# A wait for sixteen small transfers, moved from inside a group of products to the front of a dense group ahead of it

## The chip, the cores and the metric

The kernel runs on one core of a Trainium2 chip. Its engines are TensorE (matrix products into PSUM), VectorE, ScalarE, GpSimd and SyncE, each with an instruction stream of its own; they meet through semaphores. The metric is the device time of one execution in microseconds, and of several runs their median.

## What is computed

The input x has 16 images of 56 x 56 pixels with 384 channels, in float32. Two layers follow one another:

```python
x = x + L0_conv(gn(x), w_qkv, w_out, b_out, rel_pos_table)   # attention in shifted windows of 7 x 7
x = x + L1_conv(gn(x), w)                                    # 3 x 3 convolution of each channel alone
```

`gn` is a group normalization over 32 groups. In the first layer the image is rolled by 3 pixels, `q, k, v` come from one product with `w_qkv`, are cut into 12 heads of 32 channels and into windows of 49 pixels, and for each head and window

```python
score = einsum("qd,kd->qk", q, k) / sqrt(32) + rel      # some windows are masked at the image's edges
out   = einsum("qk,kd->qd", softmax(score), v)
```

is projected with `w_out`. The change concerns how `v` comes to the second of these products.

## The kernel before

**Tiling.** An image has 8 strips of 7 rows, each strip 8 windows. The 16 images give 128 strips. A strip is worked on in two units of four windows, so there are 256 units; unit u belongs to strip u // 2, and units with an even number are the first of their strip. Channels lie on the partitions in three blocks of 128.

**Order of the work.** The whole program is written out by hand: each engine does its instructions in the order in which the code issues them. `heavy` (L937) lists the work of one unit in six slots, mainly for TensorE. In the even unit of strip s it holds, for the strip after it, s + 1:

- slots 0, 1, 2: `value(s + 1, m)` (L481), the products that make v of channel block m: three products of 128 x 128 x 392 into one PSUM bank, which ScalarE then copies to `vt`.
- slots 1, 2, 3: `turn(s + 1, m)` (L494), a transpose of 32 x 32 blocks by VectorE from `vt` to `vq`, which brings keys onto partitions.
- slots 3, 4, 5: `query_key(s + 1, m)` (L469), the first three of the six blocks of q and k.
- behind slot 3 and behind slot 5: `by_key(s + 1, part)` (L501), eight DMAs each on SyncE's queue (L508). They bring `vq` into `v` of the strip, with the 49 keys of a window on consecutive partitions. Each DMA holds the values of one head in four and of one group of 32 keys. `v` has two buffers.

In the odd unit the slots hold the other three blocks of `query_key` for s + 1, then `project` (L647), the output projection of the finished strip s into `py`; VectorE adds x to it (L664) and takes its statistics (L670).

`all_units` (L971) goes through the units. Behind slot 0 of each it puts the rest of the attention of this unit: `add_up` (L589), 32 small product passes that sum the exponentials (L597); `invert` (L631), where ScalarE (L635, L636) and VectorE (L637, L638) invert the sums; `attend` (L606), 96 passes of small products of 49 x 32 x 49 with `v` (L617); and `divide` (L641). So the products with `v` of strip s in its even unit stand behind the first value group of strip s + 1, and they are some six slots and a whole unit behind the issue of the DMAs that fill `v` of strip s. Scores for the next unit (`scores`, L513) and its softmax (L535, L543, L558) come behind slot 2 or 3.

**Work between.** `at` (L899) puts further work into slots by hand-set due times: the loads of the next image (`fetch_halves`, `turn_halves` L435, `arrange` L440 with copies by ScalarE and statistics at L452) and the convolution of the image before: `band` (L698, a DMA on SyncE's queue), `pad` (L733), eight `tap`s for each chunk on VectorE (L780, L784), a transpose in place (`turn_sum`, L788, L791) and eight DMAs for each chunk out to memory (`store`, L793, L798), again on SyncE's queue. That queue issues in the program's order.

**Waits.** The framework gives each engine and each of eight DMA lanes a semaphore, and sets a wait wherever an instruction depends on another engine's or a DMA's work that its engine has not waited for yet. The sixteen DMAs of a strip are spread over the eight lanes. In the kernel before, the first eight products of `attend` in the even unit wait for the DMAs that carry their own head and keys.

Of the kernel before, what the change touches and what calls it, by code (L numbers as in the profile page):

```python
# [34 lines left out]
def kernel(  # L35
# [12 lines left out]
    nc = tc.nc  # L48
# [42 lines left out]
    def bank(name):  # L91
        return ps.tile([P, 512], F32, tag="mm", name=name)
# [388 lines left out]
    def value(s, m):  # L481

        pv = bank(f"pv_{s}_{m}")
        for c in range(NC):
            nc.tensor.matmul(  # L485
                pv[:, :ST].rearrange("p (w t) -> p w t", t=T),
                wq_t[:, c, 2 * C + m * P : 2 * C + (m + 1) * P],
                xn[:, c, :, :T],
                start=(c == 0),
                stop=(c == NC - 1),  # L490
            )
        nc.scalar.copy(vt[:, m, :, :T], pv[:, :ST].rearrange("p (w t) -> p w t", t=T))  # L492

    def turn(s, m):  # L494
# [3 lines left out]
            vt[:, m].rearrange("p (n w) (j b) -> p n (w j) b", w=2, b=D),  # L498
        )

    def by_key(s, part):  # L501

        if part == 0:
            vs[s] = vpool.tile([P, NW // 2, C], F32, tag="v", name=f"v_{s}")
        v = vs[s]
        for half in range(2 * part, 2 * part + 2):
            for i in range(HPC):
                nc.sync.dma_start(  # L508
                    v[half * D : (half + 1) * D].rearrange("k n (m c) -> k (n m) c", m=NC)[:, :, i * D : (i + 1) * D],
                    vq[i * D : (i + 1) * D, half].rearrange("k n m d -> k (n m) d"),  # L510
                )

    def scores(u, fast):  # L513


        s, n = divmod(u, UPS)
        pp = ps_s.tile([P, HPC, 512], F32, tag="s", name=f"ps_{u}")
        for j in range(NC):
            for w in range(2):
                for r in range(2):  # L520
                    for i in range(HPC):
                        part = slice(i * D, (i + 1) * D)
                        q0 = (n * UW + 2 * r + w) * T
                        row, col = (w, r) if fast else (r, w)
                        k0 = (2 * j + col) * T
                        nc.tensor.matmul(  # L526
                            pp[row * HT : (row + 1) * HT, i, k0 : k0 + T],
                            qk[part, NC * fast + j, q0 : q0 + HT],
                            qk[part, NC * (not fast) + j, q0 : q0 + T],
                            start=True,  # L530
                            stop=True,
                        )
        raw[u] = pp
# [403 lines left out]
    def heavy(u):  # L937

        s, half = divmod(u, UPS)
        todo = [[] for _ in range(2 * NC)]  # L940
        more = s + 1 < B * NS
        for m in range(NC):
            if half == 0 and more:
                todo[m].append((value, (s + 1, m)))
                todo[m + 1].append((turn, (s + 1, m)))
                todo[NC + m].append((query_key, (s + 1, m)))
            if half and more:
                todo[m].append((query_key, (s + 1, NC + m)))
            if half:
                todo[NC + m].append((project, (s, m)))  # L950
        if more and not half:
            for part in range(2):
                todo[NC + 2 * part].append((by_key, (s + 1, part)))
        if half and s + 2 < B * NS:
            todo[NC + 1].append((normalize, (s + 2,)))
        return todo
# [14 lines left out]
    def all_units(fast):  # L971
# [4 lines left out]
        for m in range(NC):  # L976
            value(0, m)
# [4 lines left out]
        for part in range(2):  # L982
            by_key(0, part)
# [142 lines left out]
```

## Time and profile before

| | |
|---|---|
| median of 3 runs | 4131.12 us |
| lowest and highest run | 4129.32 and 4135.01 us |
| profiled execution (its span; the page tells no other time of it) | 4128.7 us |
| busy: TensorE, VectorE, ScalarE, GpSimd | 4041.2, 3495.7, 2237.9, 1875.3 us |
| TensorE's clock over the span | 0.99 of full |
| values, L485: products and mean of one | 2304 passes, 497 ns |
| products with the values, L617 | 24576 passes, 212 ns |
| transfers of the values, L508 | 2048, of 48 KB |

Instructions overlap on TensorE, so that the duration of one small product says little of what it adds to the time. The distance from the start of one group to the start of the next says more, and the timeline has it. A semaphore step (EVENT_SEMAPHORE) counts as no busy time.

### The profile page before, as it was taken

How to read it: one execution, taken by the hardware profiler on the slowest of the kernel's cores; microseconds unless marked ns; L12 is line 12 of the kernel's file. 1: busy time of each engine (PE TensorE's matmuls, PEld its weight loads, DVE VectorE, ACT ScalarE, POOL GpSimd, SP SyncE). 2: the span in 40 equal slices, each digit the busy share in tenths (PEclk: the TensorE clock that was granted, in tenths of full speed). 3: DMA queues.
4: the chain of work that ended last, by engine and by line, in shares of the span. 5: the costliest groups of instructions: out<-in, count | busy, mean ns of one | idle time of the engine just before them, and what ended most of it. 6: DMA issues, size and time to landing. Idle time of an engine off the chain costs nothing.

```text
span 4128.7 us, 153178 instructions
## 1 busy us (share of the span) xinstructions
PE 4041.2 (98%) x67257; PEld 2554.0 (62%) x67257; DVE 3495.7 (85%) x3711; ACT 2237.9 (54%) x4654; POOL 1875.3 (45%) x3165
## 2 busy tenths in 40 slices
PE   5999999999999999999999999999999999999997
PEld 3666666666666666666666666666666666666656
DVE  4555989889898998989889898988989889898897
ACT  2545646555565655655555564655556555564552
POOL 5444435545453554445445453554545455452000
PEclk8999999999999999999999999999999999999998
DMA  4434556555665665556555555665556565554544
GB/s 94 79 60 90 110 100 126 105 109 103 116 114 108 116 113 103 110 98 127 106 115 108 109 116 103 117 115 100 114 100 121 104 122 109 101 121 77 107 100 109
DMA packets 1524022, 439.45 MB, mean 106 GB/s; under 512 B 1458970, under 2 KB 1473979, under 8 KB 1523346
## 3 DMA queue, kind: packets, MB, share of 16 engines
q1 hardware_dynamic: 1432680, 267.66, 38.1%
q0 software_dynamic: 87648, 159.12, 15.7%
q8 instruction: 531, 8.70, 0.9%
q10 hardware_dynamic: 3018, 2.78, 0.3%
q14 instruction: 145, 1.19, 0.1%
HBM read 169.63 MB, written 158.46 MB: 79 GB/s over the span
## 4 chain that ended last, share of the span: by engine, by line
PE 68%; issue 10%; DVE 9%; POOL 7%; DMA 4%; ACT 1%; SPq 1%; DVEq 0%; ACTq 0%; POOLq 0%
PE pq L472 28%; PE pv L485 14%; PE py L656 13%; PE ps L526 6%; PE po L617 5%; POOL xl L419 5%; DVE o L784 4%; PE ps L597 3%; DMA xl<-in_x_dram 1%; DMA mvd<-mv 1%; DVE e L543 1%; SPq L508 1%; POOL dev L268 1%; DVE st L452 1%; DVE y L664 1%
## 5 line engine op out<-in xcount | busy, mean ns | idle before, releaser
L472 PE MATMUL pq<-xn,wq_t 128*128 128x392 f32 x4608 | 1587.5, 497 | 0.1
L419 POOL DMA_DIRECT2D xl<-in_x_dram x1980 | 1331.2, 722 | 162.1 <-DVE xt L436 99.6
L784 DVE SCALAR_TENSOR_TENSOR o<-hp,dw_t,o 128x1568 f32<-128x1568 f32 x752 | 1378.4, 1833 | 5.4
L472 PEld LDWEIGHTS pq<-xn,wq_t 128*128 128x128 f32 x4608 | 846.6, 188 | 596.5 <-issue 1.9
L485 PE MATMUL pv<-xn,wq_t 128*128 128x392 f32 x2304 | 814.5, 497 | 4.7 <-DVE y L664 3.5
L656 PE MATMUL py<-ot,wo_t 128*128 128x392 f32 x2304 | 816.1, 499 | 3.0 <-DVE ot L645 3.0
L479 ACT COPY qk<-pq 128x392 f32<-128x392 f32 x768 | 369.9, 483 | 661.1 <-PE pq L472 660.1
L676 POOL COPY y<-y 128x63 f32<-128x63 f32 x128 | 54.5, 426 | 1314.6 <-DVE y L664 1314.6
L656 PEld LDWEIGHTS py<-ot,wo_t 128*128 128x128 f32 x2304 | 427.4, 190 | 298.0 <-DVE ot L645 6.9
L485 PEld LDWEIGHTS pv<-xn,wq_t 128*128 128x128 f32 x2304 | 423.6, 188 | 304.1 <-DVE y L664 5.3
L561 ACT ACTIVATE e<-e 128x1176 f32<-128x1176 f32 x256 | 303.2, 1185 | 417.9 <-DVE e L543 416.9
L637 DVE SCALAR_TENSOR_TENSOR ln<-ps,inv 128x588 f32<-128x588 f32 x256 | 195.9, 765 | 386.0 <-ACT inv L636 381.2
L492 ACT COPY vt<-pv 128x392 f32<-128x392 f32 x384 | 189.3, 493 | 431.6 <-PE pv L485 430.9
L526 PEld LDWEIGHTS ps<-qk 32*64 32x64 f32 x24576 | 308.5, 131 | 144.3 <-issue 123.0
L617 PE MATMUL po<-e,v 49*32 49x49 f32 x24576 | 368.9, 212 | 8.8 <-DMA v<-vq 7.9
L617 PEld LDWEIGHTS po<-e,v 49*32 49x32 f32 x24576 | 357.9, 105 | 16.4 <-issue 8.8
L543 DVE SCALAR_TENSOR_TENSOR e<-ps,bias 128x1176 f32<-128x1176 f32 x256 | 347.3, 1357 | 14.2 <-PE ps L526 13.9
L526 PE MATMUL ps<-qk 32*64 32x49 f32 x24576 | 340.7, 225 | 1.7 <-DVE ln L637 1.6
L448 ACT COPY x<-xt 128x196 f32<-128x196 f32 x720 | 225.6, 368 | 173.8 <-DVE xt L436 173.6
L496 DVE STREAM_TRANSPOSE vq<-vt 128x512 f32<-128x512 f32 x384 | 265.8, 693 | 8.9 <-ACT vt L492 5.4
L664 DVE TENSOR_TENSOR y<-py,x 128x392 f32<-128x392 f32 x384 | 213.2, 555 | 51.2 <-PE py L656 47.9
L461 ACT ACTIVATE xn<-x,coef 128x392 f32<-128x392 f32 x384 | 247.1, 711 | 14.5 <-DMA coef<-cod 14.5
(173 smaller groups left out, 3349.6 us busy)
## 6 DMA issues: line engine op xcount, KB each, us to landing
v<-vq SPq DMA_DIRECT2D x2048, 48.0 KB
xb<-mid SPq DMA_DIRECT2D x90, 855.5 KB
out_dram<-o SPq DMA_DIRECT2D x736, 98.0 KB
mid<-y POOLq DMA_DIRECT2D x112, 619.5 KB
xl<-in_x_dram POOLq DMA_DIRECT2D x1260, 52.5 KB
mid<-y POOLq DMA_DIRECT2D x15, 354.0 KB
xl<-in_x_dram POOLq DMA_DIRECT2D x180, 28.0 KB
mid<-y POOLq DMA_DIRECT2D x15, 265.5 KB
```

The source lines that it names most:

```text
L419: nc.gpsimd.dma_start(xz[i * D + lo : i * D + hi, c, k : k + n, :], flat[token : token + n * (hi - lo)].rearrange("(k t) c -> t k c", k=n) ...
L472: nc.tensor.matmul(pq[:, :ST].rearrange("p (w t) -> p w t", t=T), wq_t[:, c, m * P : (m + 1) * P], xn[:, c, :, :T], start=(c == 0), stop=( ...
L479: nc.scalar.copy(qk[:, m, :ST], pq[:, :ST])
L485: nc.tensor.matmul(pv[:, :ST].rearrange("p (w t) -> p w t", t=T), wq_t[:, c, 2 * C + m * P : 2 * C + (m + 1) * P], xn[:, c, :, :T], start= ...
L496: nc.vector.transpose(vq[:, :, :, m].rearrange("p h n d -> p n h d"), vt[:, m].rearrange("p (n w) (j b) -> p n (w j) b", w=2, b=D),)
L526: nc.tensor.matmul(pp[row * HT : (row + 1) * HT, i, k0 : k0 + T], qk[part, NC * fast + j, q0 : q0 + HT], qk[part, NC * (not fast) + j, q0 ...
L543: nc.vector.scalar_tensor_tensor(e, pp[:, :, : NC * 2 * T].rearrange("q i (n k) -> q i n k", k=T), QSCALE, bias[:, int(s % NS == NS - 1)]. ...
L561: nc.scalar.activation(flat, flat, AF.Exp, accum_out=reach[:, 0, u : u + 1])
L617: nc.tensor.matmul(po[w][i * D : (i + 1) * D, (2 * j + r) * T : (2 * j + r + 1) * T], vs[s][keys, n * 2 + r, h * D : (h + 1) * D], by_head ...
L656: nc.tensor.matmul(py[:, :ST], wo_t[:, c, m * P : (m + 1) * P], ots[s][:, c, :], start=(c == 0), stop=(c == NC - 1),)
L664: nc.vector.tensor_tensor(view.rearrange("p r (w c) -> p w r c", c=WIN), py[:, :ST].rearrange("p (w r c) -> p w r c", r=WIN, c=WIN), xs[s] ...
L784: nc.vector.scalar_tensor_tensor(acc, by_half(hp[:, dy : dy + BR, dx : dx + W]), dw_t[:, c, t : t + 1], acc, ALU.mult, ALU.add)
```

## The change

The DMAs of `by_key` are written down by strip. When the first product of a strip's values is issued (`c == 0` of the first block m), it is given a dependency on all sixteen DMAs of the strip before, that is, of the strip whose products with the values follow behind this group. This holds from the third strip's values on (`s > 1`). The first strip's products keep their waits, and so do the last strip's, which have no value group ahead of them.

```diff
             stop=(c == NC - 1),
             )
+            if c == 0:
+                for name in carried.pop(s - 1, ()) if s > 1 else ():
+                    tc.add_manual_dep(
+                        product.ins,
+                        name,
+                        mybir.DependencyInfo(mybir.DependencyClass.Sync, mybir.DependencyReason.DATA),
+                        reason="values of the strip ahead",
+                    )
...
+    carried = {}
 
     def by_key(s, part):
...
-                nc.sync.dma_start(
+                move = nc.sync.dma_start(
                     v[half * D : (half + 1) * D].rearrange("k n (m c) -> k (n m) c", m=NC)[:, :, i * D : (i + 1) * D],
                     vq[i * D : (i + 1) * D, half].rearrange("k n m d -> k (n m) d"),
                 )
+                carried.setdefault(s, []).append(move.ins.name)
```

No instruction changes its place in any engine's order, and no buffer changes.

More of the change, by code (lines that the diff above doesn't have):

```diff
@@ L484, in value @@
         for c in range(NC):
-            nc.tensor.matmul(
+            product = nc.tensor.matmul(
                 pv[:, :ST].rearrange("p (w t) -> p w t", t=T),
```

## The prediction

> **What bounds the kernel now.** I read the page first, then the groups of line L617, then the timelines of TensorE, of SyncE's DMA queue and of VectorE. The page says which engine sets the time:
>
> ```profile
> PE 4041.2 (98%) x67257; PEld 2554.0 (62%) x67257; DVE 3495.7 (85%) x3711; ACT 2237.9 (54%) x4654; POOL 1875.3 (45%) x3165
> L485 PE MATMUL pv<-xn,wq_t 128*128 128x392 f32 x2304 | 814.5, 497 | 4.7 <-DVE y L664 3.5
> L617 PE MATMUL po<-e,v 49*32 49x49 f32 x24576 | 368.9, 212 | 8.8 <-DMA v<-vq 7.9
> ```
>
> TensorE is busy 98% of the span and hardly ever idle in front of the values (L485) or the products with them (L617), so a microsecond given to or taken from its stream is a microsecond of the kernel. But busy is not the same as fast: a sequencer that steps through waits in the middle of overlapping small products leaves no idle time in this view. The answer for line L617 shows such steps:
>
> ```profile
> L617 PEldq EVENT_SEMAPHORE  x949: 51/51/51, 87.9 to 4012.4; - x190
> ```
>
> The timeline of TensorE in the strip that starts at 2006 prices them. Both of its units do the same 32 sums (L597) and 96 products (L617); only the first unit meets the new strip's values:
>
> ```profile
> 2006.33 2.14 PE L485 MATMUL pv<-xn,wq_t 128*128 128x392 f32 x6
> 2008.39 0.73 PE L597 MATMUL ps<-e,ones 49*32 49x147 f32 x32
> 2008.93 1.66 PE L617 MATMUL po<-e,v 49*32 49x49 f32 x96
> 2010.51 4.22 PE L485 MATMUL pv<-xn,wq_t 128*128 128x392 f32 x12
> ...
> 2024.01 0.73 PE L597 MATMUL ps<-e,ones 49*32 49x147 f32 x32
> 2024.54 1.28 PE L617 MATMUL po<-e,v 49*32 49x49 f32 x96
> 2025.75 4.22 PE L472 MATMUL pq<-xn,wq_t 128*128 128x392 f32 x12
> ```
>
> From the first sum to the next dense group: 2.12 us in the even unit, 1.74 us in the odd one. That 0.38 us is what the waits cost. All 949 wait steps lie in even units (8 in 98 strips, 6 in 13, 7 in one, 5 in 16); the odd units have none, so the program drops a wait that TensorE has already passed.
>
> The other question is when the transfers land, seen against the place where the change puts the wait. SyncE's queue in the strip whose values start at 1944.40, and TensorE's first weight load of the next strip's values:
>
> ```profile
> 1961.85 5.77 SPq L508 DMA_DIRECT2D v<-vq  x8
> 1967.66 3.01 SPq L798 DMA_DIRECT2D out_dram<-o  x4
> 1970.71 6.30 SPq L508 DMA_DIRECT2D v<-vq  x8
> ```
> ```profile
> 1975.21 1.83 PEld L485 LDWEIGHTS pv<-xn,wq_t 128*128 128x128 f32 x6
> ```
>
> The last of the sixteen transfers is issued at about 1976.4 and its semaphore is full at 1978.57, both after the group that is to wait for them has begun. The reader is to see that this needs no theory of the hardware: the wait is put ahead of the issue. Why they are late is in VectorE's timeline:
>
> ```profile
> 1951.19 0.73 DVE L637 SCALAR_TENSOR_TENSOR ln<-ps,inv 128x588 f32<-128x588 f32 x1
> 1961.12 0.67 DVE L496 STREAM_TRANSPOSE vq<-vt 128x512 f32<-128x512 f32 x1
> 1965.13 0.77 DVE L637 SCALAR_TENSOR_TENSOR ln<-ps,inv 128x588 f32<-128x588 f32 x1 [0.21 <-ACT inv L636]
> ```
>
> VectorE runs without a gap up to the third turn (1961.12), 16.7 us after the strip's start, and SyncE issues in order: eight transfers, four stores of the convolution, eight transfers. In the strip of 2006.00, where VectorE has no backlog, the first transfer starts 12.3 us in.
>
> **What the Trainium skill says.** (1) "Perfetto Trace Analysis", Identifying Dependency Chains: an instruction that waits for several engines may get EventSemaphore instructions with the further conditions ahead of it. The trace agrees: those are the 949 steps of 51 ns. (2) "TensorE: Matmul & The Clock Gate", table at its head: TensorE's queue is 64 deep. The trace agrees in kind: the one such step that the values already have stands at 2002.12, 3.9 us ahead of its product, under queued dense products. (3) "DMA: Bandwidth & Descriptors", Rules for kernel authors: issue early and wait on the semaphore late. The change waits earlier than before. (4) The TensorE page, Part 1: after an idle window of about 3.4 us the clock falls to half. The trace's clock records stand at 0.5 from 88.7 to 98.9 us, behind a 5.4 us wait for the same transfers.
>
> **The change part by part.** Durations are of the profiled execution (span 4128.7 us; the runs' median is 4131.12, so 2.4 us is added for what lies around it).
>
> *Removed: the waits inside the products*, in 126 strips (the first keeps them, the change starts at the second; the last has no value group after it). Measured from the first sum to the last product's end, medians: 2.18 us with 8 steps, 2.03 with 7, 1.92 with 6, 1.80 with 5; 1.81 in odd units. So five steps hide under the sums and each further one costs about 0.12 us. Sum over the 126: 37.7 (96 strips with 8) + 1.6 + 0.2 + 0.1 = **39.5 us**. It contains the few short waits for late landings in there. Bounds: 37 (96 x 0.37 + 13 x 0.11), and 44 if measured to the start of the next dense group.
>
> *Added: the wait steps in front of the values.* Eight semaphores, so four to eight steps of 51 ns, at most 0.4 us. Ahead of them are twelve queued passes of the output projection (L656), 4.2 us of work. Where the landings are there, they cost nothing; without that cover it would be 126 x 0.4 = 50 us, which the step at 2002.12 speaks against.
>
> *Added: the wait itself.* Queued behind it on TensorE is everything: values, sums, products, scores. For each of 126 strips I took the last semaphore update of its sixteen transfers and the start of the next strip's first value weight load. **53 are late, by 88.5 us in sum**: 23 by under 1 us, 10 by 1 to 2, 8 by 2 to 3, 12 by 3 to 3.9. In 18 even the issue begins after TensorE is there. It follows the convolution's place in a batch (8 strips): medians for strips 0 to 7 -5.2, +0.7, +1.5, -0.7, 0.0, +3.2, -3.3, -1.9 us (plus is late). Until now the products came 2.9 us after that point and most of the lateness lay under the first value group and the sums. With the median landing (2.17 us behind the issue) for all the sum is 78.
>
> *Does a stall help the next strip?* Stalled by d, TensorE starts its next value group d later, while VectorE works off its backlog, so the next transfers are less late by up to that backlog: what stands between the first unit's inverse (ScalarE) and L637 is 0.03 to 2 us. Against this TensorE arrives 0.37 us sooner from the faster products. Carried from strip to strip with these numbers the sum is 90.7; with no carry 88.5, with full carry into one next strip 91.7. The pattern explains it: the big deficits stand before strips with room. I take **88**.
>
> *Restart.* From a semaphore's last update to the product behind a wait step the trace has some 135 ns (update, step's end 79 ns later, weight load, product), and a cold first dense product takes 597 instead of 490 ns; the weight load that I count from leads its product by 0.33 us, which hides most. Up to three more steps: 0.1 us x 53 = **5 us** (0 to 10).
>
> *Clock.* Some 20 stalls are over 2 us. The trace has a 2.25 us idle stretch (4037.6 to 4039.9) with the half clock from 4041.3, and a 3.04 us one (4080.4 to 4083.4) without. A half-clock window of 3.4 us costs 1.7 us. None to twenty of them: 0 to 34 us; I take five, **8 us**, since the dense work on both sides fills part of each window.
>
> *Moved or untouched.* No DMA, copy or turn is moved, and no queue is passed; `add_manual_dep` changes waits alone. What is late next after the products: 13 times value group two waited for VectorE's eviction (3.5 us in all); in a stalled strip that is past by then, so I cost it at nothing; if not, at most 13 x 0.37 = 5 us of the gain is lost.
>
> Sum: 4128.7 - 39.5 + 88 + 5 + 8 + 2.4 = 4192.6; I say **4193 us**, 1.5% slower.
>
> **Rivals.** *Carry-over (faster).* If the room that one stall gives VectorE and SyncE stayed for the strips after, a few stalls would put the transfers ahead for good. With 3.9 us once: 4131 - 39.5 + 4 = 4096. It decides when over 55% of the lateness goes (1 - 39.5/88.5), at under 0.31 us of stall per strip. For it: VectorE is gapless for 19 us in late strips. Against: in each strip of two batches that I read, it stands idle before the odd unit's L637 (0.2 to 4.8 us, ended by ScalarE's inverse of TensorE's sums), so its lead is reset once a strip. *Once a batch.* If carry-over lasts for one batch, its largest deficit (3.4 us) counts 15 times: 51 us, and 4131 + 51 - 39.5 = 4143. *The clock decides.* Every stall over 2 us draws a window: 4131 - 39.5 + 88 + 10 + 34 = 4224, or 4240 with a few second windows. *It doesn't do what it says.* The waits stay in the products beside the new ones: 4131 + 88 + 5 + 8 = 4232; the odd units, without any wait, speak against. *Covered.* What the stalls cost is just what the products save: 4131.
>
> **How the numbers follow.** Forecast 0.70; carry-over 0.08; once a batch 0.06; clock 0.09; waits stay 0.04; covered 0.03. A difference under 0.2% (8 us) can't be told from none here. Faster 0.08, same 0.03, slower 0.89. The forecast's own bounds: low 4131 - 44 + 75 = 4162; high 4131 - 37 + 91 + 10 + 20 = 4215. The range reaches down to 4160 and up to 4232, over the clock's case and the stayed waits; left out are carry-over, once a batch and covered, 0.17.
>
> **What would show it.** Right: no wait steps in L617 and its even block at 1.28 us as the odd one; idle time of TensorE before L485, ended by v<-vq, some 50 times, near 90 us, longest about 4, at the same places in each batch; VectorE idle for longer before L637; SyncE's transfers at the same distance behind L496. Wrong: idle time before L485 under 40 us (carry-over), steps left in L617, or the granted clock at 0.5 far more than ten times. The prediction falls if the stalls of a batch shrink from strip to strip.

## The result, and the profile after

The changed kernel takes 4184.39 us in the median of four runs (4174.46 to 4185.65), against 4131.23 us (4129.32 to 4135.01) before: a ratio of 1.0123, with a 95% interval from 1.0109 to 1.0138. The change makes the kernel 1.2% slower. The profiled execution, with a span of 4172.7 us, is the shortest of the four; the others took 9 to 11 us more and were granted a mean clock of 0.984 to 0.985 instead of 0.986. One to two thousandths of 4182 us are 4 to 8 us, so more time at the half clock can be most of that; this is an estimate, since only the first has a trace.

The page of the changed kernel, the lines that answer to those of before. After the bar stand the busy time in us, the mean of one in ns, and the idle time ahead with what ended most of it:

```profile
PE 4016.4 (96%) x67257; PEld 2507.7 (60%) x67257; DVE 3497.5 (84%) x3711; ACT 2238.8 (54%) x4654; POOL 1862.2 (45%) x3165
L485 PE MATMUL pv<-xn,wq_t 128*128 128x392 f32 x2304 | 835.7, 507 | 77.6 <-DMA v<-vq 47.5
L628 PE MATMUL po<-e,v 49*32 49x49 f32 x24576 | 311.8, 213 | 8.5 <-DMA v<-vq 7.8
L648 DVE SCALAR_TENSOR_TENSOR ln<-ps,inv 128x588 f32<-128x588 f32 x256 | 196.2, 767 | 435.7 <-ACT inv L647 431.8
```

Two things move in opposite directions. The products with the values (now L628) are busy for 57 us less, with the same 24576 passes. In front of the values TensorE idles for 77.6 us, where it idled for 4.7. VectorE waits 50 us longer ahead of L648 than it did at L637 before the change:

```profile
L637 DVE SCALAR_TENSOR_TENSOR ln<-ps,inv 128x588 f32<-128x588 f32 x256 | 195.9, 765 | 386.0 <-ACT inv L636 381.2
```

It waits for ScalarE's inverse of sums that TensorE, itself waiting, delivers later.

Where the wait steps went, from the groups of L628 and L485 with the change, and of L485 before it (duration in ns: least, median, most):

```profile
L628 PEldq EVENT_SEMAPHORE  x16: 51/51/51, 86.4 to 4056.1; - x16
```
```profile
L485 PEldq EVENT_SEMAPHORE  x631: 51/51/5242, 74.0 to 4021.4; - x158
```
```profile
L485 PEldq EVENT_SEMAPHORE  x127: 51/51/51, 75.6 to 3975.9; - x127
```

Of 949 steps in the products 16 are left, those of the first and the last strip. The values have 631 instead of 127, four more in each of 126 strips: one step can carry two semaphores. The longest, at 3362.18, takes 5.2 us: there the sequencer really waits. But for 4.2 us from 3362.06 on TensorE still runs the projection that is queued, and stands idle for 1.5 us only, so the length of a step is not the loss.

A strip without a late landing, on TensorE's timeline of the changed kernel (start, duration, then the instructions):

```profile
2029.76 2.14 PE L485 MATMUL pv<-xn,wq_t 128*128 128x392 f32 x6
2031.83 0.73 PE L608 MATMUL ps<-e,ones 49*32 49x147 f32 x32
2032.36 1.14 PE L628 MATMUL po<-e,v 49*32 49x49 f32 x96
2033.44 4.22 PE L485 MATMUL pv<-xn,wq_t 128*128 128x392 f32 x12
...
2046.93 0.73 PE L608 MATMUL ps<-e,ones 49*32 49x147 f32 x32
2047.46 1.14 PE L628 MATMUL po<-e,v 49*32 49x49 f32 x96
2048.53 4.22 PE L472 MATMUL pq<-xn,wq_t 128*128 128x392 f32 x12
```

The even unit's products take 1.14 us instead of 1.66.

And the strip ahead of it, whose transfers come late: SyncE's queue first, then TensorE. (By the code, seven to nine slots lie between the issue of the transfers and the products that read them: what is left of the even unit, the odd unit's six and slot 0. That is less than the six slots and a whole unit named above.)

```profile
1980.32 6.27 SPq L518 DMA_DIRECT2D v<-vq  x8
1986.63 2.69 SPq L809 DMA_DIRECT2D out_dram<-o  x4
1989.36 6.36 SPq L518 DMA_DIRECT2D v<-vq  x8
```
```profile
1989.96 4.22 PE L667 MATMUL py<-ot,wo_t 128*128 128x392 f32 x12
1997.59 3.91 PE L485 MATMUL pv<-xn,wq_t 128*128 128x392 f32 x6 [3.42 <-DMA v<-vq]
2001.43 0.73 PE L608 MATMUL ps<-e,ones 49*32 49x147 f32 x32
```

TensorE has finished the projection at 1994.2 and stands for 3.4 us, until the transfers issued last (up to 1995.7) have landed. Then the six value passes take 3.91 us where they took 2.14: after the stall they run at half the clock. The busy time by windows shows it. Behind the busy times of the five engines stand PEclk, the granted clock, with 0.62 against 1.00, then the DMA engines' busy share and GB/s:

```profile
1997.00:2001.50 4.50, 3.91 (x14) 1.77 (x21) 1.07 (x1) 0.00 (x0) 2.07 (x3) 0.62 0.70 188
2029.70:2033.50 3.80, 3.80 (x136) 2.54 (x134) 3.35 (x4) 1.28 (x3) 3.24 (x8) 1.00 0.96 144
```

### The profile page after: what moved, and what is told of

Same layout as the page of the kernel before. It is cut to its first block, busy times and chain, and to the rows that moved or that the text cites. A ratio compares the mean times of both kernels' runs of the same rounds, so it can differ in the third digit from the quotient of the medians.

```text
span 4172.7 us, 152749 instructions
## 1 busy us (share of the span) xinstructions
PE 4016.4 (96%) x67257; PEld 2507.7 (60%) x67257; DVE 3497.5 (84%) x3711; ACT 2238.8 (54%) x4654; POOL 1862.2 (45%) x3165
## 4 chain that ended last, share of the span: by engine, by line
PE 43%; issue 19%; POOL 14%; DVE 9%; DMA 8%; SPq 6%; ACT 1%; DVEq 0%; ACTq 0%; POOLq 0%
PE pq L472 17%; PE pv L485 10%; POOL xl L419 10%; PE py L667 7%; SPq L518 4%; DVE o L795 4%; PE ps L537 3%; PE po L628 3%; PE ps L608 2%; DMA mvd<-mv 2%; DMA xl<-in_x_dram 2%; DMA mid<-y 1%; DVE e L554 1%; SPq L809 1%; POOL dev L268 1%
## 5 line engine op out<-in xcount | busy, mean ns | idle before, releaser
L485 PE MATMUL pv<-xn,wq_t 128*128 128x392 f32 x2304 | 835.7, 507 | 77.6 <-DMA v<-vq 47.5
L485 PEld LDWEIGHTS pv<-xn,wq_t 128*128 128x128 f32 x2304 | 426.3, 191 | 398.6 <-issue 98.0
L648 DVE SCALAR_TENSOR_TENSOR ln<-ps,inv 128x588 f32<-128x588 f32 x256 | 196.2, 767 | 435.7 <-ACT inv L647 431.8
L628 PE MATMUL po<-e,v 49*32 49x49 f32 x24576 | 311.8, 213 | 8.5 <-DMA v<-vq 7.8
L628 PEld LDWEIGHTS po<-e,v 49*32 49x32 f32 x24576 | 304.5, 105 | 13.1 <-issue 9.2
```

Of the source, the lines that this page charges most:

```text
L485: product = nc.tensor.matmul(pv[:, :ST].rearrange("p (w t) -> p w t", t=T), wq_t[:, c, 2 * C + m * P : 2 * C + (m + 1) * P], xn[:, c, :, : ...
L628: nc.tensor.matmul(po[w][i * D : (i + 1) * D, (2 * j + r) * T : (2 * j + r + 1) * T], vs[s][keys, n * 2 + r, h * D : (h + 1) * D], by_head ...
```

## The theories and the experiments

**Theory A**: the loss is the late landings at the new place, the gain is a block of products free of wait steps; the gain can be had without the loss. **Theory B**: the price is that of the wait steps themselves, now ahead of a dense group, or of the place whatever the landings. **Theory C**: the time is set by SyncE's and VectorE's side alone. In what follows "the block" is the stretch from the first product of the sums to the end of the products with the values in an even unit, and "the wait" the time by which a strip's first value product starts later than the usual 0.329 us behind the start of the product before it; both are sums over 126 strips, read from the trace's single instructions. (The idle time of the page is a little less than the wait, because an idle stretch is counted only from the end of the product before.) Before, they are 267.5 and 0.0 us; with the change 214.1 and 82.9 us. Each time is told with that of the kernel before on the same chip.

### Wait at the sums

The sixteen transfers are waited for at the first product of `add_up`, not at the first value product (shown against the changed kernel, shortened).

```diff
-            if c == 0:
-                for name in carried.pop(s - 1, ()) if s > 1 else ():
-                    tc.add_manual_dep(product.ins, name, ...)
@@ def add_up(u): @@
+                    if u % UPS == 0 and u >= UPS:
+                        for name in carried.pop(u // UPS, ()):
+                            tc.add_manual_dep(product.ins, name, ...)
```

> The sixteen transfers are waited for at the first product of the sums, some 2.4 us behind the place of the change and still ahead of the products with the values. Theory A (the change loses by late landings at its place, and gains by a block of products free of wait steps): the block stays at 1.67 us in even units, against the kernel before this gives 53 us; of the landings 18 are still late, by 15 us in sum; some 4131 - 53 + 17 = 4095 us, faster than before. Theory B (the price is paid for the wait steps that now stand ahead of a dense group, or for the half clock whatever the wait's length): the steps are as many here, so the time stays near 4170 to 4185 us. Theory C (VectorE's and SyncE's part alone sets the time): no change against the changed kernel, 4184 us.

Measured: 4115.81 us against 4131.28, ratio 0.9962 (0.9948 to 0.9976). The block is 219.8 us, median 1.67, as theory A says; the wait is now between the values and the sums, 23 us. So 2.4 us later the waits for the same transfers turn a loss of 53 us into a gain of 15. That speaks against theory B; the next run settles it, at the place of the change itself.

The gain is 20 us smaller than I expected, and 27 us smaller in the traced execution, which took 5 us more than the median. There 6 us are more waiting, 5 us the block, and 11 us second value groups under six stretches of 3.4 us at half the clock, which I had not counted. Another 7 us are waits of the second value group for VectorE's eviction (10.0 us instead of 3.5), not counted either.

### The first eight alone

```diff
-                carried.setdefault(s, []).append(move.ins.name)
+                if part == 0:
+                    carried.setdefault(s, []).append(move.ins.name)
```

> At the place of the change, but only the first eight transfers of the strip are waited for there; the last eight keep their waits inside the products. In the trace of before the first eight are never late at that place (3.1 us of room at the least). Theory A: no stall in front of the values, four wait steps left in the products, which hide under the sums as the first four of eight did; 53 us less than before plus some 4 us of late landings inside, about 4082 us. Theory B: wait steps ahead of the values cost as before, so 4160 us or more. If each step left costs 0.125 us without cover: 4131 - 53 + 126 x 0.5 = 4141 us.

Measured: 4103.86 us against 4131.28, ratio 0.9938 (0.9921 to 0.9954). The place, and the number of steps there, are those of the change:

```profile
L485 PEldq EVENT_SEMAPHORE  x631: 51/51/304, 75.0 to 3949.3; - x158
```

but nothing is late, the longest step is 0.3 us, the wait is 0.0 and the stretch from the values to the sums is 260.6 us in sum, to the tenth what it was before. Wait steps ahead of a dense group cost nothing here, and theory B falls. The four steps left in the products do cost: the block is 235.4 us, median 1.80 instead of 1.67, so they aren't hidden entirely, and I had expected them to be. That is 17 us of the 22 by which the expectation missed; 6 us more went to VectorE's eviction (`y`, L676), for which the second value group now waits 9.4 us instead of 3.5.

### The transfers in a row

The second eight DMAs are issued right behind the first eight, so that no store and no load of a convolution band stands between them on SyncE's queue; once on the changed kernel, once on the kernel before.

```diff
-                todo[NC + 2 * part].append((by_key, (s + 1, part)))
+                todo[NC].append((by_key, (s + 1, part)))
```

> The changed kernel with the second eight transfers issued right behind the first eight (behind slot 3 instead of slot 5), so that no store or band load stands between them on SyncE's queue. Worked out on the trace of before, the last landing is then 0.07 us or more ahead of the place of the wait in every strip. Theory A: nearly all of the 83 us of stalls goes, the block free of waits stays: 4131 - 53 + 5 = 4083 us, up to 4095 us if TensorE's earlier arrival makes a few landings late again. Theory C (VectorE's turns alone make the landings late): SyncE's order changes little, 4165 to 4184 us.

Measured: 4104.01 us against 4131.28, ratio 0.9932 (0.9915 to 0.9948). The page of the values:

```profile
L485 PE MATMUL pv<-xn,wq_t 128*128 128x392 f32 x2304 | 819.3, 499 | 25.4 <-DVE y L675 11.1
```

The wait falls from 82.9 to 17.4 us, 24 times over 0.2 us and at most 2.2. The block is 213.0 us. SyncE's order alone thus takes away 65 of 83 us. Theory C's prediction of 4165 us or more fails. What is left is more than the working promised (none late). Most of that was wrong in the working itself: in the trace of the next run, where TensorE keeps its old pace, some 25 last landings are already late against the same place, by 11 us in sum. That TensorE comes earlier by half a microsecond a strip may account for the rest. Waits for VectorE's `y` rose to 11 us.

> The kernel before with the second eight transfers behind the first eight, all waits inside the products as before. Theory A: the wait steps stay (block 2.18 us), only the few microseconds of late landings inside the products go: 4124 to 4131 us, same as before. If instead the transfers' order is worth something by itself (stores delayed, queue freed), more than 8 us in either direction.

Measured: 4139.73 us against 4131.28, ratio 1.0023 (1.0013 to 1.0032): slower by 8 us, which I didn't expect. The groups of its line L617 tell why:

```profile
L617 PEldq EVENT_SEMAPHORE  x1024: 51/51/51, 87.4 to 4021.2; - x171
```

1024 steps instead of 949. The transfers go round eight DMA semaphores. Before, 30 of the 126 strips had one, two, three or five other DMAs between the two eights, and these have five to seven steps; strips with none or with four between have eight. With all sixteen in a row every strip has eight. The block rises from 267.5 to 276.0 us, the whole 8 us. Without meaning to, this run measured the steps a second time.

### Fewer taps

Four of eight taps of each convolution chunk are left out for the first fifteen images, so their convolution is incomplete. VectorE has less to do ahead of the turns.

```diff
             for i, t in enumerate((0, 1, 2, 3, 5, 6, 7, 8)):
-                at(when + step * i / 9, tap, p, k, c, t)
+                if i % 2:
+                    at(when + step * i / 9, tap, p, k, c, t)
```

> The changed kernel with four of the eight taps of each convolution chunk left out for the first fifteen images (their convolution is incomplete; the last image has all), which takes some 650 us of work off VectorE. Theory A: the landings are late at the new place because VectorE's backlog delays the third turn, so with the backlog gone the waits in front of the values all but vanish and what stays is the block free of wait steps: 53 us less than the kernel before, less some 7 us that the second value group then waits for VectorE's eviction: about 4085 us. Theory C (SyncE's order of issue alone makes them late, whatever VectorE does): 20 us or more of waits stay, 4105 us or more. Theory B (steps ahead of the values, or the mere place of the wait, cost): 4160 us or more.

Measured, on the changed kernel: 4121.61 us against 4133.18, ratio 0.9969 (0.9956 to 0.9981). The wait is 39.1 us, half of 82.9, where theory A in the form that I had given it expected almost none. VectorE's backlog is a cause, but not the only one. (With the taps out TensorE also loses 12 us among the products of the scores in the traced execution, with no wait that the profile shows; the expectation had no such term.)

> The kernel before with the same four of eight taps left out (first fifteen images, their convolution incomplete). TensorE sets its time, so taking work off VectorE gives nothing but the few waits for it: 4118 to 4133 us. Then the changed kernel with these taps left out (4121.61 us) stands as its trace says: free block -53, waits in front of the values +39, half clock and restarts +7. If VectorE bounded the kernel: over 100 us less.

Measured, on the kernel before: 4135.02 us against 4130.70, ratio 1.0008 (1.0001 to 1.0015).

```profile
PE 4048.3 (98%) x67257; PEld 2560.3 (62%) x67257; DVE 2889.5 (70%) x3351; ACT 2251.7 (54%) x4654; POOL 1758.9 (42%) x3165
```

Taking 606 us of work off VectorE gives nothing, so VectorE doesn't bound the kernel before, and theory C falls. In the trace the second value group waits 4.4 us less, and the products of the scores take 15 us more; what delays them stays open.

Both causes together, taps out and the transfers in a row, on the changed kernel:

> The changed kernel with both causes of late landings taken away: four of eight taps left out (first fifteen images, their convolution incomplete) and the second eight transfers right behind the first eight. Two causes in a row (VectorE's backlog ahead of the first transfer, SyncE's stores between the eights): the waits in front of the values, 83 us in the changed kernel, 39 with the taps out, 17 with the transfers in a row, go to 0 to 3 us; 4080 to 4095 us. If a third cause were left, 10 us or more of waits stay.

Measured: 4071.25 us against 4130.70, ratio 0.9854 (0.9838 to 0.9871), with part of the work left out: 9 us below the range that I had expected. The wait is 0.7 us in all, and the waits for VectorE's `y` are gone too. So two causes stand in a row ahead of the landing: VectorE delays the first transfer, what SyncE issues between the eights delays the last. With both the wait is 83 us, with VectorE's backlog alone 17, with SyncE's order alone (and half the taps) 39, with neither 0.7. The two single ones sum to less than both together, because a landing is late only beyond its room.

### All waits at the first product with the values

The kernel before, with its DMAs written down as in the change (shortened):

```diff
@@ def attend(u, fast): @@
+                        if n == 0 and s > 0:
+                            for name in carried.pop(s, ()):
+                                tc.add_manual_dep(product.ins, name, ...)
```

> All waits of the strip gathered at the first product with the values, 2.9 us behind the place of the change, instead of spread over eight products. Some 20 landings are late there by 10 to 15 us in sum, since TensorE comes sooner than before. If four steps in a row hide under the sums: block 1.67 to 1.80 us, 30 to 48 us less than before, together 4095 to 4115 us. If steps of 0.125 us are not hidden there: block about 2.2 us as before and 4131 to 4145 us.

Measured: 4099.22 us against 4130.70, ratio 0.9920 (0.9903 to 0.9936). The steps are gathered, half as many, and in front of the first product instead of among the first eight. The block's median is 1.67 us, as without steps; late landings, now inside it, bring its sum to 229.6:

```profile
L620 PEldq EVENT_SEMAPHORE  x516: 51/51/1912, 88.5 to 3984.0; - x172
```

So four steps in a row ahead of the products hide under the sums that are still running; the same number spread among the products, in the run with the first eight alone, cost 0.13 us a strip. The gain could be had here without moving the wait ahead of the dense group.

### In a row, and waited for at the sums

What the runs point to: no store between the transfers, and the wait 2.4 us later than the change has it.

> Both improvements: the second eight transfers behind the first eight, and the wait at the first product of the sums. Theory A: no late landing is left (the kernel with the transfers in a row had a longest wait of 2.2 us in front of the values, the sums begin 2.4 us later), steps hidden under the value group, block at 1.67 us: 4131 - 54 + 8 (second value group waits for VectorE's eviction) = 4085 us, the fastest of all. If the gain of the free block and the earlier wait for VectorE cancel further: 4100 us, as with the transfers in a row or the first eight alone.

Measured: 4092.51 us against 4133.18, ratio 0.9901 (0.9884 to 0.9917), the fastest complete kernel of the study, 2% below the changed one in ratio to the kernel before. Its page:

```profile
PE 3990.7 (98%) x67257; PEld 2501.7 (61%) x67257; DVE 3496.3 (85%) x3711; ACT 2232.2 (55%) x4654; POOL 1863.0 (46%) x3165
L485 PE MATMUL pv<-xn,wq_t 128*128 128x392 f32 x2304 | 817.5, 498 | 11.9 <-DVE y L675 10.7
L628 PE MATMUL po<-e,v 49*32 49x49 f32 x24576 | 312.7, 213 | 11.8 <-DMA v<-vq 7.8
```

TensorE is busy 98% again, the block is 215.7 us, and between the values and the sums 1.2 us are lost in all. It misses 4085 us by 7; the waits for VectorE's `y` (10.7 us instead of 3.5) were in the sum already. In the trace the rest is many small terms: 2 us the block, 1.8 us one stretch at half the clock, 1.2 us in front of the sums, and some 3 us in and just ahead of the projection and among the scores.

## Why the prediction was right, point by point

From the first value product of the third strip to that of the last, the trace of before has 3855.7 us and that of after 3900.4, so 44.7 us are to be explained, of which the terms name all but 0.9:

| term | forecast | measured |
|---|---|---|
| waits leave the products | -39.5 | -57.1 |
| late landings in front of the values | +88 | +82.9 |
| restart behind a stall | +5 | +2.9 |
| half clock | +8 | +18.8 |
| all else in and behind the blocks of products | 0 | -3.7 |
| sum | +61.5 | +43.8 |

- **The place of the late landings** was right: 44 waits over 0.2 us (forecast 53 late), 82.9 us in sum, at most 4.5. The medians by place in a batch were +0.7, +1.5 and +3.2 us late at the three bad places, and TensorE waited 1.0, 1.0 and 3.2 us there. In the trace of the change the last of the sixteen landings stands 0.3 us (median) ahead of the first weight load at each of these places, so it is what ended the wait. (The page names `v<-vq` for 47.5 of its 77.6 us of idle time, and for the rest other work that ended at nearly the same time.) At the second place the sum fell from 24.5 to 13.5 us and at the first it rose from 12.7 to 20.4. Both fit the working (a stall one strip ahead lets VectorE come nearer; TensorE comes sooner), and they nearly cancel as it said; no run takes the two apart.
- **The waits leave the products**: right in kind and 17.6 us too small. I took the odd unit, 1.81 us, for a block without any loss. It isn't one. A free block takes 1.67 us, as 109 of the 126 even units do with the change. The odd unit has no wait steps, but in most strips one gap of some 60 to 150 ns among its products, at a changing place and with no wait that ends there; what makes it stays open. In steps of 0.125 us, the usual distance from one to the next in the trace, 2.18 - 1.67 = 0.51 us makes four of eight steps hidden and four paid, not five and three. The measured term is 267.5 - 126 x 1.67 = 57.1 us.
- **The steps ahead of the values** cost nothing, as costed, with the 4.2 us of projection as their cover; the run with the first eight alone shows it.
- **Restart** was 2.1 us too large. I had read 597 ns as the first dense product after a pause. It is the first pass behind the small products, and takes that long in every strip of the kernel before, none of which stalls; behind a stall at full clock the first pass takes 567 or 568 ns in 40 strips.
- **The clock** was the term most in doubt, and 10.8 us too small. Sixteen idle stretches of TensorE in front of the values are over 2 us, and in or behind ten of them the clock falls to a half for 3.4 or 6.8 us: 17.0 us in ten value groups and 1.8 us in the blocks of four of these strips.
- **Carry-over as a rival** (4096 us) and the once-a-batch form (4143 us) are out: the stalls come back in every batch, 2.7 to 4.5 us at the same place in nearly all of them. The stayed waits are out with the 16 steps left in L628.

The mechanism was right and the sum less so: on the traces it is 17.7 us too high, since the gain was 17.6 us too small and the clock's 10.8 us in the other direction made up for no more than the other three terms. The forecast of 4193 us lies within 9 us of the measured median only because the three runs without a trace took 9 to 11 us more than the traced one. That is luck and not working.

## What to carry to other kernels

In these runs a wait cost by where its last event landed against where it stood, not by how tidy the group behind it was; before moving one ahead, lay the landing beside the new place strip by strip, and follow the queue that issues the transfers, which here held up to four stores between them. Steps through waits already satisfied were free under queued dense products and in a row ahead of small ones. Among overlapping small ones they cost 0.125 us each beyond the first four of eight, and four of them 0.13 us together. The reference for "no waits" must be read from a block that has none, not from its neighbour.

## What the runs showed of the hardware that was not expected

The half clock comes after shorter idle than the Trainium skill, "TensorE: Matmul & The Clock Gate", Part 1, suggests with an idle window of about 3.4 us: behind 2.85 and 2.87 us in the changed kernel, and behind 1.36 and 1.60 us where all waits stand at the first product with the values, each time for 3.4 us; while 3.67 us in the changed kernel drew none. The first two lines are the 1.36 us and the window behind it (clock 0.51), the last two the 3.67 us (clock 1.00). The view names a store as what ended both; the last of the strip's own sixteen transfers landed at 493.62 and at 3493.94, about half a microsecond ahead:

```profile
494.06 1.08 PE L620 MATMUL po<-e,v 49*32 49x49 f32 x96 [1.36 <-DMA out_dram<-o]
495.30:498.70 3.40, 3.40 (x6) 1.75 (x6) 3.30 (x4) 2.18 (x3) 0.39 (x2) 0.51 0.71 211
3494.50 2.21 PE L485 MATMUL pv<-xn,wq_t 128*128 128x392 f32 x6 [3.67 <-DMA out_dram<-o]
3494.50:3497.90 3.40, 3.40 (x111) 2.28 (x114) 0.44 (x1) 0.91 (x2) 1.44 (x3) 1.00 0.53 162
```

A stall thus has an uncertain surcharge, here 18.8 us over ten of sixteen stalls, which the sum of waits doesn't show. The number of wait steps depends on how the DMAs fall on the eight semaphores: 949 or 1024 for the same transfers, worth 8 us.
